# Batch-norm sums in a graph network kernel: the squares and sums of a pair of tiles move one pair later in the order

## The chip, the cores and the metric

The kernel runs on one core of one Trainium2 chip. The metric is device microseconds of one execution. Before the change three runs took 1545.77, 1546.34 and 1549.16 us, so the median is 1546.34 us. The engines are named as in the profile: PE is TensorE (with PEld for its weight loads), DVE is VectorE, ACT is ScalarE, POOL is GpSimd, SP is SyncE, whose queue issues most DMA transfers.

## The reference

The input is a matrix x of 6250 nodes by 256 features and 200,000 edges (src, dst). The part that matters here is the end of it, the batch norm over the nodes and the layer norm of each row:

```python
gc = m @ W_gc + b_gc                       # m: normalised sum over a node's edges
x = gc + (feats @ W_res + b_res)
core = _moe_ff(x, Wg, bg, w1, b1, w2, b2)  # top 2 of 64 experts: g1*y1 + g2*y2 per node
y = x + core
mean = jnp.mean(y, axis=0)
var = jnp.mean((y - mean) ** 2, axis=0)
gnn = (y - mean) * jax.lax.rsqrt(var + BN_EPS) * gamma + beta
out = _layernorm(feats + gnn, axis=-1)
```

The mean and the variance run over all 6250 nodes, so no output row can be finished before the last row of y is known.

## The kernel before, in words

The nodes are cut into NT = 50 tiles of TP = 125 rows. The sums over the edges, the linear layers, the routing and the 64 experts come first and take the span up to about 1418 us. The experts write their results to DRAM (y_dram), two rows of 256 numbers for each node. The pre-expert x of all nodes lies in SBUF in one tile, `x_all`, 125 partitions by 50 by 256, float32.

Then comes the part that the change touches, which I call the batch-norm part. It goes over the 50 tiles in 25 pairs (t0 = 0, 2, 4, ...). For each pair the order in the code is:

- SP issues the load of the pair's expert results from y_dram into a buffer `yr` (512 KB; two loads of half a pair for the first two pairs). There are 8 such buffers, and the loads of later pairs wait until DVE has read the buffer eight pairs before.
- ACT multiplies each tile's second expert row by its gate, in place (L1576, two instructions).
- DVE multiplies each tile's first expert row by its gate and adds it to x (L1578, two instructions), and then adds the gated second rows of both tiles (L1580, one instruction of 512 columns).
- ACT squares the finished pair into a buffer `sq` (L1582, one instruction of 512 columns; 4 such buffers).
- PE adds up x over the 125 rows with a matmul against a matrix of ones, accumulating in PSUM in `pm` (L1584), and likewise `sq` in `pv` (L1586). Each is two matmuls per pair in the code, and each of these stands as two in the trace, so `pm` and `pv` show four matmuls each per pair.

These blocks stand in a `manual_schedule`, which keeps each engine's instructions in the order of the code. An engine works its own list strictly from the front: an instruction that waits holds up everything behind it on that engine. Between engines only the semaphores of the data order the work.

After the last pair the mean is taken from `pm` (L1588), then the variance from `pv` (L1592), and from them `scale` and `less` (L1593 to L1598). The last part (L1622 to L1654) scales every tile, adds the input and the batch norm's shift, does the layer norm and writes the rows out, in groups of up to five tiles. It needs `scale`, so all of it stands behind the sums.

Of the kernel before, what the change touches and what calls it, by code (L numbers as in the profile page):

```python
# [9 lines left out]
F32 = mybir.dt.float32  # L10
# [16 lines left out]
TP = 125  # L27
NT = N // TP
# [3 lines left out]
D = 256  # L32
# [117 lines left out]
def gnn_moe_kernel(ctx, tc, x_in, x_cols, src, dst, bases, nexts, firsts, parts, lasts, W_gc, b_gc, W_res, b_res, Wg, bg, w1, b1, w2, b2,  # L150
# [31 lines left out]
    def node_in(tile_ap, ap, t0, n, end=NT):  # L182

        if t0 + n in (end, NT):
            node_dma(nc.sync, True, tile_ap[:TP, n - 1:n], node_rows(ap, t0 + n - 1, 1))
            n -= 1
        if n:
            loads.append(nc.sync.dma_start(out=tile_ap[:, :n], in_=bass.AP(  # L188
                tensor=ap.tensor, offset=ap.offset + t0 * TP * ap.ap[0][0],
                ap=[[ap.ap[0][0], 128], [TP * ap.ap[0][0], n], [1, ap.shape[1]]])))  # L190
# [1362 lines left out]
    with tc.tile_pool(name="fin", bufs=1) as fp, tc.tile_pool(name="gat", bufs=8) as gp, \  # L1553
# [10 lines left out]
        S.activation(eps[:, 1:2], eps[:, 0:1], AF.Sqrt)  # L1564
        pm = ps_m.tile([TP, D], F32, name="pm")
        pv = ps_m.tile([TP, D], F32, name="pv")
        for t0 in range(0, NT, 2):
            yr = gp.tile([128, 2, 2, D], F32, name="yr")
            for t in range(t0, t0 + 2) if t0 < 4 else (t0,):
                n = 1 if t0 < 4 else 2  # L1570
                loads.clear()
                node_in(yr[:, t - t0:t - t0 + n].rearrange("p t j d -> p t (j d)"), y_rows, t, n)
                for u in written[-AHEAD:-1] if t == 0 else ():
                    tc.add_manual_dep(loads[0].ins, u.name, SYNCED, reason="the last writes")
            for t in range(t0, t0 + 2):
                S.activation(yr[:TP, t - t0, 1, :], yr[:TP, t - t0, 1, :], AF.Copy, scale=gates[:, 1, t:t + 1])  # L1576
            for t in range(t0, t0 + 2):
                V.scalar_tensor_tensor(x[:, t, :], yr[:TP, t - t0, 0, :], gates[:, 0, t:t + 1], x[:, t, :],  # L1578
                                       op0=ALU.mult, op1=ALU.add)
            V.tensor_tensor(x[:, t0:t0 + 2, :], x[:, t0:t0 + 2, :], yr[:TP, :, 1, :], ALU.add)  # L1580
            sq = fl.tile([TP, 2, D], F32, name="sq", bufs=4)
            S.activation(sq, x[:, t0:t0 + 2, :], AF.Square)  # L1582
            for t in range(t0, t0 + 2):
                T.matmul(pm, ones[:TP, :TP], x[:, t, :], start=(t == 0), stop=(t == NT - 1))  # L1584
            for t in range(t0, t0 + 2):
                T.matmul(pv, ones[:TP, :TP], sq[:, t - t0, :], start=(t == 0), stop=(t == NT - 1))  # L1586
        mean = fp.tile([TP, D], F32, name="mean")
        V.tensor_scalar(mean, pm, 1.0 / N, None, op0=ALU.mult)  # L1588
        msq = fp.tile([TP, D], F32, name="msq")
# [12 lines left out]
        groups, t0 = [], 0  # L1602
# [120 lines left out]
```

## Time and profile before

| quantity | value |
|---|---|
| median of three runs | 1546.34 us |
| the profiled execution's own time | 1543.25 us |
| its span, first to last instruction | 1541.5 us |
| mean granted TensorE clock over the span | 0.959 |
| batch-norm part, first gate product to first use of `pv` | 1421.19 to 1479.63 us |
| pairs in it | 25 |
| last part, from the first scaling to the end | 1483.45 to 1541.5 us |

The span is in microseconds from the first instruction. The profiled execution took 3.1 us less than the median of the runs; of its own time 1.75 us lie outside the span. In the batch-norm part the reader should look at four engines at once: ACT and DVE hand each other a pair's data twice, PE only receives, and SP's loads run ahead. POOL does nothing there.

### The profile page before, as it was taken

How to read it: one execution, taken by the hardware profiler on the slowest of the kernel's cores; microseconds unless marked ns; L12 is line 12 of the kernel's file. 1: busy time of each engine (PE TensorE's matmuls, PEld its weight loads, DVE VectorE, ACT ScalarE, POOL GpSimd, SP SyncE). 2: the span in 40 equal slices, each digit the busy share in tenths (PEclk: the TensorE clock that was granted, in tenths of full speed). 3: DMA queues.
4: the chain of work that ended last, by engine and by line, in shares of the span. 5: the costliest groups of instructions: out<-in, count | busy, mean ns of one | idle time of the engine just before them, and what ended most of it. 6: DMA issues, size and time to landing. Idle time of an engine off the chain costs nothing. (4 is left out here: it accounts for less than half of the span.)

```text
span 1541.5 us, 33071 instructions
## 1 busy us (share of the span) xinstructions
PE 1380.2 (90%) x9987; PEld 1147.4 (74%) x9987; DVE 1047.4 (68%) x2943; ACT 745.3 (48%) x1891; POOL 784.1 (51%) x878
## 2 busy tenths in 40 slices
PE   5999478899999999999999967799999999997963
PEld 3555267788888899999999956688888877875642
DVE  9999889989888888888777749333223233222687
ACT  4675544456666566665555524322222222222668
POOL 7000226777776677766666620376566665652000
PEclk9999699999999999999999978899999999998986
DMA  6899665777777787777777737478687887874804
GB/s 192 263 287 327 241 212 162 209 226 224 210 220 221 204 235 214 217 214 219 218 204 216 203 94 245 130 255 268 203 277 253 277 272 219 250 243 152 286 22 147
DMA packets 209177, 336.41 MB, mean 218 GB/s; under 512 B 22283, under 2 KB 140758, under 8 KB 208989
## 3 DMA queue, kind: packets, MB, share of 16 engines
q1 hardware_dynamic: 154201, 180.36, 37.2%
q0 software_dynamic: 47888, 146.77, 32.4%
q10 hardware_dynamic: 6900, 7.07, 1.6%
q8 instruction: 81, 1.33, 0.4%
q14 instruction: 107, 0.88, 0.2%
HBM read 254.55 MB, written 73.10 MB: 213 GB/s over the span
## 5 line engine op out<-in xcount | busy, mean ns | idle before, releaser
L613 POOL DMA_INDIRECT r<-h_dram,srcg x445 | 468.9, 1054 | 244.1 <-PE pc L699 79.4
L745 PE MATMUL sm<-hrow,counts 128*128 128x258 f32 x1470 | 486.9, 346 | 8.4 <-DVE counts L736 8.3
L719 ACT CAST counts<-pc 128x196 f32 (+7 forms) x879 | 356.9, 406 | 209.0 <-PE pc L699 175.0
L746 PE MATMUL sm<-hrow,counts 128*128 128x256 f32 x1470 | 394.6, 282 | 0.0
L699 PE MATMUL pc<-hotk,lo 128*128 128x245 bf16 (+7 forms) x1118 | 305.0, 304 | 41.7 <-DVE counts L736 19.9
L745 PEld LDWEIGHTS sm<-hrow,counts 128*128 128x128 f32 x1470 | 286.6, 195 | 26.4 <-issue 11.9
L686 DVE TENSOR_TENSOR hotk<-key,iota_h 128x784 bf16<-128x784 f16 (+4 forms) x488 | 246.8, 506 | 58.1 <-PE pc L699 56.0
L746 PEld LDWEIGHTS sm<-hrow,counts 128*128 128x128 f32 x1470 | 279.8, 190 | 1.3
L1442 ACT ACTIVATE hT<-ph,b1c 128x112 f32<-128x112 f32 (+16 forms) x256 | 109.9, 430 | 325.4 <-PE ph L1440 309.9
L736 DVE TENSOR_TENSOR counts<-pc,counts 128x49 f32 x908 | 217.6, 240 | 48.8 <-ACT counts L719 12.3
L1452 PE MATMUL py<-w2s,hT 128*128 128x256 f32 (+7 forms) x992 | 238.0, 383 | 0.0
L1440 PE MATMUL ph<-xgT,w1s 128*128 128x112 f32 (+17 forms) x1024 | 203.0, 342 | 0.6 <-DVE xgT L1430 0.6
L1452 PEld LDWEIGHTS py<-w2s,hT 128*128 128x128 f32 (+7 forms) x992 | 161.0, 170 | 42.2 <-DVE ys L1455 2.5
L1440 PEld LDWEIGHTS ph<-xgT,w1s 128*128 128x128 f32 x1024 | 167.7, 192 | 31.1 <-issue 11.2
L1405 POOL DMA_INDIRECT y_dram<-ys,dest x124 | 119.1, 960 | 112.2 <-DVE ys L1455 63.7
L1455 DVE TENSOR_TENSOR ys<-py,b2s 128x256 f32<-128x256 f32 (+7 forms) x124 | 52.3, 422 | 176.9 <-PE py L1452 167.5
L1405 POOL DMA_INDIRECT xg<-x_dram,ids x124 | 120.3, 970 | 91.9 <-DVE ids L1362 52.9
L699 PEld LDWEIGHTS <-lo 128*128 128x128 bf16 x1118 | 99.5, 100 | 74.7 <-issue 17.4
L618 PE MATMUL pg<-r,hot 128*128 128x258 f32 x445 | 144.6, 325 | 3.1 <-DMA r<-h_dram,srcg 2.3
L1430 DVE TENSOR_SCALAR xgT<-pte,bsum 128x112 f32<-128x112 f32 (+14 forms) x128 | 48.8, 423 | 125.9 <-PE pte L1427 125.8
L619 PE MATMUL pg<-r,hot 128*128 128x256 f32 x445 | 125.1, 281 | 0.0
L457 PE MATMUL pr<-wcat,f 128*128 128x512 f32 x196 | 99.6, 632 | 3.2 <-DMA wcat<-in_L_gnn_W_res_dram 3.2
(330 smaller groups left out, 1724.7 us busy)
## 6 DMA issues: line engine op xcount, KB each, us to landing
w1s<-in_L_gnn_w_dram SPq DMA_DIRECT2D x64, 512.0 KB
w2s<-in_L_gnn_w_dram SPq DMA_DIRECT2D x64, 512.0 KB
y_dram<-zeros SPq DMA_DIRECT2D x48, 256.0 KB
yr<-y_dram SPq DMA_DIRECT2D x22, 512.0 KB
b2s<-in_L_gnn_b_dram SPq DMA_DIRECT2D x64, 128.0 KB
h_dram<-hrow SPq DMA_DIRECT2D x5, 1536.0 KB
r<-h_dram,srcg POOLq DMA_INDIRECT x445
f<-in_x_cols_dram SPq DMA_DIRECT2D x25, 256.0 KB
```

The lines of the kernel that those rows point to most:

```text
L613: G.indirect_dma_start(out=f32(r[:, :2 * D]), out_offset=None, in_=h_dram[:, :], in_offset=bass.IndirectOffsetOnAxis(ap=idx, axis=0))
L618: T.matmul(pg, hot, r[:, D:], start=first, stop=False)
L619: T.matmul(pg[:, :D], hot, r[:, :D], start=False, stop=last)
L686: V.tensor_tensor(hot, pairs(key, e, n, m), iota_h[:, None, :m, :].to_broadcast([128, n // 2, m, 2]), ALU.is_equal)
L699: T.matmul(pc, los[g // PAIRS][:, r // 2, :, r % 2], hots.pop(g), start=(i == 0), stop=(i == k - 1))
L719: put = S.copy(counts[c % 2][:, :, 1:][:, :, ds(at, w - 1)], pc[:, :, 1:])
L736: add = V.tensor_tensor(to, more, f32(had), ALU.add).ins
L745: T.matmul(sm, by, hrow[:, t, D:], start=(t == 0), stop=False)
L746: T.matmul(sm[:, :D], by, hrow[:, t, :D], start=False, stop=(t == NS - 1))
L1405: w = G.indirect_dma_start(**kw)
L1440: T.matmul(ph[:, :m], w1s[:, kk, c * 128:(c + 1) * 128], xgT[:, kk, :m], start=(kk == 0), stop=(kk == 1))
L1452: T.matmul(py[:n], hT[:, c, k * 128:k * 128 + n], w2s[:, c, :], start=(c == 0), stop=(c == 3))
```

## The change

The body of the loop is cut in two functions. `joined(t0)` holds the load, the gate products and the sums with x; `summed(t0)` holds the squares and the two sums on PE. The loop now calls `joined` for a pair and then `summed` for the pair before it; the last pair's `summed` comes after the loop. Nothing is computed in another way. The squares have 3 buffers instead of 4.

```diff
-        for t0 in range(0, NT, 2):
+        def joined(t0):
+
             yr = gp.tile([128, 2, 2, D], F32, name="yr")
...
             V.tensor_tensor(x[:, t0:t0 + 2, :], x[:, t0:t0 + 2, :], yr[:TP, :, 1, :], ALU.add)
-            sq = fl.tile([TP, 2, D], F32, name="sq", bufs=4)
+
+        def summed(t0):
+
+            sq = fl.tile([TP, 2, D], F32, name="sq", bufs=3)
             S.activation(sq, x[:, t0:t0 + 2, :], AF.Square)
             for t in range(t0, t0 + 2):
                 T.matmul(pm, ones[:TP, :TP], x[:, t, :], start=(t == 0), stop=(t == NT - 1))
             for t in range(t0, t0 + 2):
                 T.matmul(pv, ones[:TP, :TP], sq[:, t - t0, :], start=(t == 0), stop=(t == NT - 1))
+
+        for t0 in range(0, NT, 2):
+            joined(t0)
+            if t0:
+                summed(t0 - 2)
+        summed(NT - 2)
```

Only ACT's list changes its order. At the start of the batch-norm part, where `yr` is the buffer of a pair's expert results (one number for each pair), `sq` the squares and "x2" two instructions alike, ACT had before:

```order
L1576 ACTIVATE yr_21471<-yr_21471,gates_16387 125x256 x2
L1582 ACTIVATE sq_21479<-x_all_16381 125x512
L1576 ACTIVATE yr_21485<-yr_21485,gates_16387 125x256 x2
L1582 ACTIVATE sq_21493<-x_all_16381 125x512
L1576 ACTIVATE yr_21499<-yr_21499,gates_16387 125x256 x2
L1582 ACTIVATE sq_21506<-x_all_16381 125x512
```

and has now:

```order
L1577 ACTIVATE yr_21471<-yr_21471,gates_16387 125x256 x2
L1577 ACTIVATE yr_21479<-yr_21479,gates_16387 125x256 x2
L1586 ACTIVATE sq_21487<-x_all_16381 125x512
L1577 ACTIVATE yr_21493<-yr_21493,gates_16387 125x256 x2
L1586 ACTIVATE sq_21500<-x_all_16381 125x512
L1577 ACTIVATE yr_21506<-yr_21506,gates_16387 125x256 x2
```

The gate products of the second pair have moved ahead of the first pair's squares, and so on for each later pair: the squares that stand behind a pair's gate products are now those of the pair before. At the end of the part, up to the square root for `scale`, ACT had before:

```order
L1576 ACTIVATE yr_21772<-yr_21772,gates_16387 125x256 x2
L1582 ACTIVATE sq_21779<-x_all_16381 125x512
L1576 ACTIVATE yr_21785<-yr_21785,gates_16387 125x256 x2
L1582 ACTIVATE sq_21794<-x_all_16381 125x512
L1594 ACTIVATE scale_21804<-scale_21804 125x256
```

and has now:

```order
L1577 ACTIVATE yr_21766<-yr_21766,gates_16387 125x256 x2
L1586 ACTIVATE sq_21773<-x_all_16381 125x512
L1577 ACTIVATE yr_21779<-yr_21779,gates_16387 125x256 x2
L1586 ACTIVATE sq_21788<-x_all_16381 125x512
L1586 ACTIVATE sq_21794<-x_all_16381 125x512
L1604 ACTIVATE scale_21804<-scale_21804 125x256
```

Here the squares of the last two pairs stand one behind the other. The lists of PE, DVE and SP hold the same instructions in the same order as before; PE's is two matmuls into `pm` and two into `pv` for each pair, 25 times. The fourth square and those after it now wait for PE to have read the squares three pairs before; it was four.

## The prediction

> **What bounds the kernel now.** I read the chain of waits first, near its end, because the change touches only a stretch close to the end of the program. Columns: start, duration (us), and what stood on the chain.
>
> ```profile
> 1467.73 0.70 DVE x_all L1580
> 1468.48 0.04 issue
> 1468.52 0.63 ACT sq L1582
> 1469.15 0.81 ACT yr L1576 x2
> 1469.96 0.02 issue
> 1469.98 0.70 DVE x_all L1580
> ...
> 1477.47 1.14 PE pm L1584 x4
> 1478.61 0.02 issue
> 1478.63 0.44 DVE mean L1588
> ...
> 1479.63 0.43 DVE scale L1592
> ```
>
> The same three steps come back for every pair: DVE finishes a pair (L1580), ACT squares it (L1582), and only then may ACT make the gate products of the next pair (L1576), which DVE waits for. From 1467.73 to 1469.98 is 2.25 us for one pair. PE is on this chain only behind the last pair, and the mean and `scale` stand directly behind PE. The last part of the kernel needs `scale`, so what the sums gain or lose moves the end of the kernel by as much.
>
> The list of waits between 1434.5 and 1477.47 us says the same in totals (us, times, longest):
>
> ```profile
> ACT sq L1582 <- DVE x_all L1580: 15.8, 19, 1.1
> DVE x_all L1580 <- ACT yr L1576: 14.8, 19, 1.1
> PE pm L1584 <- DVE x_all L1580: 5.2, 20, 0.4
> ```
>
> ACT and DVE wait for each other about 0.8 us in each of 19 pairs, and PE waits for DVE. So no engine is full: the bound is a loop of two engines. The timeline of one pair shows how much work there is apart from the waiting (start, duration, instruction; in brackets the idle time before it and who ended it):
>
> ```profile
> 1433.75 0.69 DVE L1580 TENSOR_TENSOR x_all<-x_all,yr 125x512 f32<-125x512 f32 x1 [0.76 <-ACT yr L1576]
> 1434.36 0.88 DVE L1578 SCALAR_TENSOR_TENSOR x_all<-yr,gates,x_all 125x256 f32<-125x256 f32 x2
> 1434.54 0.63 ACT L1582 ACTIVATE sq<-x_all 125x512 f32<-125x512 f32 x1 [0.82 <-DVE x_all L1580]
> 1435.08 0.89 ACT L1576 ACTIVATE yr<-yr,gates 125x256 f32<-125x256 f32 x2
> 1436.00 0.69 DVE L1580 TENSOR_TENSOR x_all<-x_all,yr 125x512 f32<-125x512 f32 x1 [0.76 <-ACT yr L1576]
> ```
>
> DVE's period is 2.25 us (1433.75 to 1436.00) with 0.76 idle: 1.49 us of work. ACT's is 2.25 with 0.82 idle: 1.43 us of work.
>
> PE's own need is read where PE was behind and worked without a gap, early in the part, from starts and not from ends:
>
> ```profile
> 1428.90 1.03 PE L1584 MATMUL pm<-x_all,ones 125*125 125x256 f32 x4
> 1429.77 1.03 PE L1586 MATMUL pv<-sq,ones 125*125 125x256 f32 x4
> 1430.63 1.03 PE L1584 MATMUL pm<-x_all,ones 125*125 125x256 f32 x4
> ...
> 1434.50 1.13 PE L1584 MATMUL pm<-x_all,ones 125*125 125x256 f32 x4 [0.25 <-DVE x_all L1580]
> ...
> 1477.47 1.13 PE L1584 MATMUL pm<-x_all,ones 125*125 125x256 f32 x4 [0.26 <-DVE x_all L1580]
> ```
>
> Four matmuls take 0.865 us, a pair 1.73 us (1428.90 to 1430.63). So the needs for one pair are PE 1.73, DVE 1.49, ACT 1.43, against 2.25 now.
>
> **The change part by part.** *ACT's order.* Nothing is added or removed; 24 of the 25 squares move behind the gate products of the next pair. The gate products of pair k+1 then no longer stand behind a square that waits for DVE's pair k. What is left of the loop is this: L1580 of pair k, the square of pair k (0.54 us from its start to the next start on ACT, 1434.54 to 1435.08), gate products of pair k+2 (0.89), L1580 of pair k+2 (0.69), with hand-overs of some 0.1: 2.2 us again, but for two pairs, so 1.1 us a pair. That is below the work of each engine alone, so the loop no longer binds. Next in line is the fullest engine, PE with 1.73 us a pair.
>
> *The main term.* The third pair's `pm` starts at 1428.90 and the 25th's at 1477.47: 48.57 us for 22 pairs. At 1.73 us these are 38.06. Gain 10.51 us.
>
> *The start.* The first square now stands behind the gate products of the second pair, and these wait for a load:
>
> ```profile
> 1423.20 0.63 ACT L1582 ACTIVATE sq<-x_all 125x512 f32<-125x512 f32 x1 [0.80 <-DVE x_all L1580]
> 1424.36 0.48 DVE L1578 SCALAR_TENSOR_TENSOR x_all<-yr,gates,x_all 125x256 f32<-125x256 f32 x1 [0.61 <-DMA yr<-y_dram]
> 1423.22 2.07 PE L1584 MATMUL pm<-x_all,ones 125*125 125x256 f32 x4 [9.45 <-DMA yr<-y_dram]
> 1425.09 1.91 PE L1586 MATMUL pv<-sq,ones 125*125 125x256 f32 x4
> 1426.80 1.41 PE L1584 MATMUL pm<-x_all,ones 125*125 125x256 f32 x4
> ```
>
> The second half of pair 2 lands for 1424.36. Its gate product takes 0.4 to 0.5 us (two take 0.89), so the first square starts at about 1424.8 instead of 1423.20 and ends at 1425.4. The first `pv` matmuls, now at 1425.09, start at about 1425.5: PE stands 0.4 us in its list, with everything behind it. PE is slow there anyhow, as its clock shows (columns: window, length, PE busy, granted clock, DMA share, GB/s):
>
> ```profile
> 1426.00:1427.00 1.00, 1.00 (x4) 0.50 0.97 299
> 1427.00:1428.00 1.00, 1.00 (x4) 0.72 1.01 356
> 1428.00:1429.00 1.00, 1.00 (x6) 1.00 1.07 416
> ```
>
> The clock doubles within 1427 to 1428, at about 1427.56 by its mean of 0.72. If it steps at the same time, the 0.4 us of slow work that was put off is done at twice the speed later and costs 0.2. Bounds: 0 (the first pair may be fed in time) and 0.4 (the step moves along). I take 0.2. Between 1428.90 and the end nothing else is late: the later pairs' gate products and squares run at 1.43 to 1.49 us a pair and PE at 1.73, so the lead grows.
>
> *Three buffers of squares in place of four.* ACT's square of pair k waits until PE has read that of pair k-3; behind it on ACT stand the gate products of pair k+2, and DVE's L1580 waits for those. From that release to a finished pair k+2 are 0.54 + 0.89 + 0.69 and about 0.1 for the hand-overs, 2.2 us; PE then still has pairs k-2 to k+1 before it, 4 x 1.73 = 6.9 us. The wait holds ACT and DVE back to PE's pace and PE never sees it. Cost 0. Even a single buffer would leave it two pairs, 3.5 us, as cover; without any the wait would cost up to 2.2 us a pair.
>
> *The loads.* Their number and order on SP's queue stay; the pace at which buffers come free changes.
>
> ```profile
> 1430.00:1440.00 10.00, 9.24 (x41) 7.03 (x40) 6.74 (x15) 6.68 (x15) 0.00 (x0) 1.00 1.05 390
> 1440.00:1450.00 10.00, 8.95 (x37) 6.19 (x35) 6.46 (x13) 6.17 (x14) 0.00 (x0) 1.00 0.77 261
> ...
> SPq L188 <- DVE x_all L1580: 25.7, 15, 1.8
> ```
>
> These rows end in clock, DMA share and GB/s. With buffers free the loads move 390 GB/s. From 1440 on it is 261, and SP's queue waits 25.7 us for DVE to give buffers back, so it is DVE that slows them. A pair of 512 KB (524,288 bytes) takes 1.34 us at 390 and would need 303 GB/s at 1.73 us. Cost 0. If 261 were all that the loads can give, a pair would take 2.0 us from about the 14th pair on; the eight buffers' lead of some 5 pairs over the work covers most of it, and I bound this cost at 11 x (2.0 - 1.73) = 3.0 us.
>
> *The end.* The last pair's L1580 and square are done several us before PE gets to them, so the mean follows PE's last `pm` as it does now. The last part keeps its order. Cost 0.
>
> *Sum.* 10.5 - 0.2 = 10.3 us. The profiled execution, 1543.25 us (span 1541.5), would become 1532.9. It took 3.1 us less than the median of the runs, and no part of that lies in an edit here, so I take the 10.3 off the median: 1546.3 - 10.3 = 1536.0 us, 0.7%.
>
> The row of waits above says that PE idles for only 5.2 us in this stretch, and a reader could take that for all there is to win. The gap of 0.25 us is counted from the modelled end of the matmul before, which shows a latency (four matmuls 1.03 us long start 0.865 apart); the starts tell the pace. The Trainium skill (Perfetto Trace Analysis, section Tensor Engine Instruction (MATMUL, LD_WEIGHTS)) says of these records that the profiler computes the end from the size of the instruction and does not observe it. By starts the sum is 10.5, by the idle rows 5.2; this case's rows agree with the page, since consecutive records overlap.
>
> **The rivals.**
>
> *The clock steps up later.* PE's 0.4 us of idleness falls into the stretch in which the clock is still 0.50. If the wait for full clock began anew at 1425.5, it would last as long as the first time (1423.22 to 1427.56, 4.3 us), until 1429.8: 2.3 us more at half speed, which cost 1.1 us, and with the 0.4 us the gain would be 10.5 - 1.5 = 9.0: 1537.3 us. For it speaks only that PE was busy without a gap before the step in the trace; against it, that 0.4 of 4 us is little. The Trainium skill (TensorE: Matmul & The Clock Gate, section What's actually happening) states that the clock steps up after one busy window of about 3.4 us that runs freely, not counted from the first matmul; by it the step comes at the same time or one window later, for which half of 3.4, an estimate of 1.7 us, would be lost. The 4.3 us from first matmul to step agree with such a window, and no run here shows what a gap in it does.
>
> *The idle rows are right.* If a matmul behind a full queue took the 0.1 us longer that the records after a wait show, PE would need 2.25 - 0.25 = 2.0 us a pair and the gain would be 5.2 less the start: 5.0, so 1541.3 us. Against it: the groups quoted from 1428.90 on start 0.865 us apart, each behind a full queue.
>
> *The loads hold PE up* by the bound above: gain 7.3, so 1539.0 us. Against it: 390 GB/s while buffers were free.
>
> *Slower: the half clock stays.* At clock 0.50 four matmuls take 1.71 us (1425.09 to 1426.80), a pair 3.42. If the broken start left PE at half clock, each us of it would cost half a us, so the gain is gone when the half clock lasts some 20 us longer; if it lasted the whole part, 22 x (3.42 - 2.21) = 26.6 us would be lost: 1573 us. Against it: a PE that is fuller than now, and rows like this one of the middle of the kernel, where PE worked 200 us without a gap at full clock:
>
> ```profile
> 600.00:800.00 200.00, 200.00 (x1544) 188.87 (x1544) 161.85 (x533) 121.78 (x267) 135.67 (x131) 1.00 0.75 214
> ```
>
> *It does not do what it says.* If the squares still stood ahead of the next gate products, nothing would move: 1546. The instruction order excludes that for ACT; what could still do it is a wait that asks for more than its data.
>
> **How the numbers follow.** The forecast, with the start at 0 to 0.4 us, has 0.78. The later clock has 0.07, the loads 0.06, the idle rows 0.04, no effect 0.03, slower 0.02. The predicted time is 1536.0 us. The three runs before lie within 3.4 us, so a median of few runs may be off by 1 to 2 us: the range goes from 1533.5 (gain 10.5 and a low median) to 1539.0 (takes in the later clock and the loads' bound). The chances: a measurement of this kernel tells about 0.2%, 3 us, from no change. All cases but the last two gain more: faster 0.95. No effect stays within it: same 0.03. Slower 0.02.
>
> **What would show it.** Right: the chain no longer has the square between L1580 and the gate products; PE stands on it from the first pairs to the mean; `pm` starts 1.73 us apart from the third pair on; DVE's first use of `pv` comes about 10.3 us earlier after the first gate product than the 58.4 us now (1421.19 to 1479.63); ACT's squares wait for PE in the second half. The start is right if the first `pv` matmul comes 0.3 to 0.5 us later and the clock still steps within the same us. Wrong: `pm` starts 2.0 us apart or more at clock 1.00 (idle rows), gate products that wait for loads after the third pair (loads), a clock of 0.50 beyond 1428.5 (later clock), or a last part that grows.

## The result and the profile after

The changed kernel takes 1535.49 us in the median of six runs (1533.3 to 1537.3), the kernel before 1546.76 us in the median of six (1544.88 to 1549.16). The ratio is 0.9925 with a 95% interval of 0.991 to 0.9939, so the gain is 9 to 14 us. A second comparison on one chip, five runs of the changed kernel against nine of the one before, gave 1537.74 against 1547.12 us, ratio 0.9937 (0.9924 to 0.9951).

The chain of waits in the batch-norm part, in the profiled execution after (start, us, what):

```profile
1422.38 5.26 DMA yr<-y_dram
1427.67 0.51 ACT yr L1577
1428.17 0.53 ACT sq L1586
1428.70 0.04 issue
1428.75 2.07 PE pv L1590 x4
1430.82 0.86 PE pm L1588 x4
1431.68 0.86 PE pv L1590 x4
...
1469.67 0.86 PE pv L1590 x4
1470.53 0.88 PE pm L1588 x4
1471.43 0.44 DVE mean L1598
...
1472.43 0.44 DVE scale L1602
```

The three steps of DVE and ACT that came back in every pair are gone from the chain. From the first `pv` to the mean the chain is PE alone, 0.86 us for each group of four matmuls. The timeline of PE gives the pace by starts:

```profile
1426.26 2.07 PE L1588 MATMUL pm<-x_all,ones 125*125 125x256 f32 x4 [9.91 <-DVE x_all L1581]
1428.75 2.07 PE L1590 MATMUL pv<-sq,ones 125*125 125x256 f32 x4 [0.41 <-ACT sq L1586]
1430.61 1.07 PE L1588 MATMUL pm<-x_all,ones 125*125 125x256 f32 x4
1431.52 1.03 PE L1590 MATMUL pv<-sq,ones 125*125 125x256 f32 x4
1432.38 1.03 PE L1588 MATMUL pm<-x_all,ones 125*125 125x256 f32 x4
...
1470.37 1.03 PE L1588 MATMUL pm<-x_all,ones 125*125 125x256 f32 x4
```

From the third `pm` (1432.38) to the 25th (1470.37) are 37.99 us, 1.727 a pair; before it was 48.57. The windows show PE full, DVE and ACT at most 95% busy, and the loads at 390 GB/s for longer than before (columns: window, length, then busy time and count of PE, PEld, DVE, ACT and POOL, granted clock, DMA share, GB/s):

```profile
1430.00:1440.00 10.00, 10.00 (x46) 8.58 (x46) 9.37 (x19) 9.51 (x21) 0.00 (x0) 0.97 1.05 392
1440.00:1450.00 10.00, 10.00 (x48) 8.68 (x47) 9.37 (x20) 8.84 (x20) 0.00 (x0) 1.00 1.05 387
1450.00:1460.00 10.00, 10.00 (x48) 8.70 (x47) 9.37 (x20) 8.42 (x18) 0.00 (x0) 1.00 0.85 287
```

DVE is closer to its own limit than the 9.37 us suggest. Its last steps of two pairs start 1.59 us apart (L1581, 1434.72 and 1436.31), and it keeps that pace until 1461.73, so it gains only 0.14 us a pair on PE.

The list of waits from 1425 to 1468 us shows what ACT waits for now:

```profile
ACT sq L1586 <- PE pv L1590: 4.0, 11, 1.1
ACT sq L1586 <- DVE x_all L1581: 1.4, 9, 0.2
DVE x_all L1581 <- ACT yr L1577: 0.4, 2, 0.2
```

ACT's and DVE's waits for each other fell from 30.6 us to 1.8 us, over 43 us each, and in 11 pairs, from 1449.85 us on, the square waits for PE to give a buffer back.

I divide the part into the start (first gate product to the third `pm`), the stretch (third to 25th `pm`), and the end (to the first use of `pv`), and put the two profiled executions side by side:

| us | before | after | difference |
|---|---|---|---|
| up to the first gate product | 1421.19 | 1423.08 | +1.89 |
| start | 7.71 | 9.30 | +1.59 |
| stretch, 22 pairs | 48.57 | 37.99 | -10.58 |
| end | 2.16 | 2.06 | -0.10 |
| last part, from the first use of `pv` to the end of the span | 61.87 | 61.87 | 0.00 |
| span | 1541.5 | 1534.3 | -7.2 |

The first row lies ahead of the change. It moves from execution to execution: in the nine profiled executions on chips on which the kernel before takes 1544 to 1547 us it came at 1421.19 to 1425.40 us. Without this row the execution after is 9.1 us shorter (7.2 and 1.9). The two profiled executions took 1543.25 and 1536.07 us, 7.2 us apart, and the medians lie 11.3 us apart; these two profiles do not show where the 2.2 us between 9.1 and 11.3 lie.

### The profile page after: what moved, and what is told of

It is laid out like the page before. It is cut to its first block, busy times and chain, and to the rows that moved or that the text cites. A ratio compares the mean times of both kernels' runs of the same rounds, so it can differ in the third digit from the quotient of the medians.

```text
span 1534.3 us, 33072 instructions
## 1 busy us (share of the span) xinstructions
PE 1376.0 (90%) x9987; PEld 1149.8 (75%) x9987; DVE 1051.2 (69%) x2943; ACT 745.3 (49%) x1891; POOL 780.8 (51%) x878
## 6 DMA issues: line engine op xcount, KB each, us to landing
h_dram<-hrow SPq DMA_DIRECT2D x5, 1536.0 KB
```

## The experiments

Each kernel was profiled once. I compare the three pieces of the part, which do not depend on how late it began. Four of the kernels (half of `pv` in the order before, two pairs behind, the first pair at once, the warm PE) ran on another chip, on which the kernel before took 1613.42 us, so only the pieces of these are used. The two kernels with half of `pv` leave the squares of every second tile out of the variance; they serve to find the bound and nothing else. The last three rows have five runs each, the rows between them and the first two a single one.

| kernel | start | stretch | us a pair | whole part |
|---|---|---|---|---|
| before | 7.71 | 48.57 | 2.21 | 58.44 |
| after | 9.30 | 37.99 | 1.73 | 49.35 |
| after, four buffers | 9.63 | 37.99 | 1.73 | 49.67 |
| before, three buffers | 8.30 | 48.85 | 2.22 | 59.30 |
| after, one buffer | 7.94 | 41.73 | 1.90 | 51.77 |
| after, half of `pv` | 7.81 | 34.64 | 1.57 | 44.61 |
| before, half of `pv` | 7.93 | 49.46 | 2.25 | 59.55 |
| after, two pairs behind | 11.74 | 37.99 | 1.73 | 51.79 |
| after, first pair at once | 8.93 | 37.98 | 1.73 | 48.97 |
| after, warm PE | 8.32 | 37.99 | 1.73 | 48.37 |
| after, once more | 11.22 | 37.99 | 1.73 | 51.27 |
| after, rounded squares | 8.56 | 34.18 | 1.55 | 44.90 |
| after, rounded squares, warm PE | 7.20 | 34.85 | 1.58 | 44.21 |

### The number of buffers, alone

```diff
-            sq = fl.tile([TP, 2, D], F32, name="sq", bufs=3)
+            sq = fl.tile([TP, 2, D], F32, name="sq", bufs=4)
```

> The changed kernel with four buffers of squares again in place of three. Theory (PE sets the pace, the buffers cost nothing): pm starts from the third to the 25th pair 38.0 us, 1.73 us a pair as with three, and ACT's squares wait for PE less often than in 11 pairs; time within 2 us of 1535.5. Rival (three buffers hold the pairs back): a shorter stretch, 36 us or less, and 1533 us or less.

The stretch is 37.99 us to the hundredth, the time 1535.47 us in one run. The square waits for PE in 2 pairs instead of 11, and that changes nothing. The reverse, three buffers in the old order:

```diff
-            sq = fl.tile([TP, 2, D], F32, name="sq", bufs=4)
+            sq = fl.tile([TP, 2, D], F32, name="sq", bufs=3)
```

> The kernel before with three buffers of squares in place of four, order unchanged. Theory (the order of ACT's list sets the pace before, not the buffers): pm starts from the third to the 25th pair 48.6 us as before, time within 2 us of 1546.5. Rival (the number of buffers has a part in the gain): a different stretch by more than 1 us.

The stretch is 48.85 us (48.57 with four), the time 1546.3 in one run. Between three buffers and four, only the order counts.

One buffer tests the reasoning of the prediction on the wait for a buffer, which had found even a single one covered:

```diff
-            sq = fl.tile([TP, 2, D], F32, name="sq", bufs=3)
+            sq = fl.tile([TP, 2, D], F32, name="sq", bufs=1)
```

> The changed kernel with one buffer of squares. The square of a pair then waits until PE has read the pair before. Theory of the prediction: from that release to the next square's end is 0.63 us and some 0.1 of hand-over, while PE has 0.86 us of pm matmuls before it needs it, so PE keeps 1.73 to 1.80 us a pair, a stretch of 38.0 to 39.6 us. Rival (the wait reaches PE): the loop of PE, square, gate products and DVE binds, 2.2 us or more a pair, a stretch of 48 us or more.

Neither: 1.90 us a pair, a stretch of 41.73 us, 1540.79 us in all. The timeline of this kernel shows the loop (DVE's lines and the weight loads left out):

```profile
1449.77 0.81 PE L1590 MATMUL pv<-sq,ones 125*125 125x256 f32 x3
...
1450.41 1.03 PE L1588 MATMUL pm<-x_all,ones 125*125 125x256 f32 x4
1450.66 0.63 ACT L1586 ACTIVATE sq<-x_all 125x512 f32<-125x512 f32 x1 [0.47 <-ACT yr L1577]
...
1451.34 1.13 PE L1590 MATMUL pv<-sq,ones 125*125 125x256 f32 x4
...
1452.56 0.63 ACT L1586 ACTIVATE sq<-x_all 125x512 f32<-125x512 f32 x1 [0.47 <-ACT yr L1577]
...
1453.24 1.13 PE L1590 MATMUL pv<-sq,ones 125*125 125x256 f32 x4
```

The brackets name ACT's own instruction before the square, but that had ended at 1450.19, 0.47 us earlier: what the square waits for is PE. The square starts 1.22 us after the start of `pv` (1451.34 to 1452.56): four matmuls that follow a wait stand at 1.13 us to their modelled end, and 0.09 us more pass until ACT starts. With 0.63 us for the square and 0.05 us to the next `pv` that is 1.90 us. The expectation had counted the matmuls at their pace of 0.86 us; who waits for them to finish has to count their length. The prediction's "two pairs, 3.5 us, as cover" for a single buffer is wrong for another reason: it followed the wait only through the gate products to the `pm` two pairs later. But the square itself is what the very next `pv` needs, and only that pair's `pm`, 0.86 us, lies between. With three buffers PE has two pairs more to do in between, and nothing of the wait shows.

### Less work on PE, in the new order and in the old

```diff
-            for t in range(t0, t0 + 2):
-                T.matmul(pv, ones[:TP, :TP], sq[:, t - t0, :], start=(t == 0), stop=(t == NT - 1))
+            T.matmul(pv, ones[:TP, :TP], sq[:, 0, :], start=(t0 == 0), stop=(t0 == NT - 2))
```

> The changed kernel without the pv matmuls of the second tile of each pair: the squares of half of the tiles are left out of the variance. PE then needs 1.30 us a pair. Theory (PE sets the pace, DVE is next): pm starts fall to DVE's pace, 1.5 to 1.6 us a pair, a stretch of 33 to 35.2 us, and DVE shows hardly any idle time. Rival (loads are next): the stretch falls less or not at all, and gate products wait for loads after the third pair. Rival (the loop of ACT and DVE still sets the pace): 38 us.

With a quarter of PE's work gone the pairs come 1.57 us apart, the stretch is 3.4 us and the part 4.7 us shorter. The timeline shows that DVE is the next bound: its instructions stand without a wait in the list, and it is PE's weight loads that wait for DVE.

```profile
1446.54 0.69 DVE L1581 TENSOR_TENSOR x_all<-x_all,yr 125x512 f32<-125x512 f32 x1
...
1447.15 0.87 DVE L1579 SCALAR_TENSOR_TENSOR x_all<-yr,gates,x_all 125x256 f32<-125x256 f32 x2
1447.28 0.72 PEld L1588 LDWEIGHTS pm<-x_all,ones 125*125 125x125 f32 x4 [0.43 <-DVE x_all L1581]
...
1448.12 0.69 DVE L1581 TENSOR_TENSOR x_all<-x_all,yr 125x512 f32<-125x512 f32 x1
```

DVE's own need is 1.58 us a pair (1446.54 to 1448.12), not the 1.49 that I had read as period less idle time. DVE's last step starts 0.97 us after the start of the two before it when it follows them directly (1447.15 to 1448.12), although these take 0.87.

The same cut in the old order, with the same edit:

> The kernel before without the pv matmuls of the second tile of each pair: the squares of half of the tiles are left out of the variance. PE's need falls from 1.73 to 1.30 us a pair. Theory (before, the loop of ACT and DVE sets the pace, PE none): 2.21 to 2.25 us a pair from the third pair to the 25th, 48.6 us or up to 1 us more since PE has no backlog to work off at the start; end of the part 0.4 us earlier at most. Rival (PE's matmuls behind a wait have a share in it): 2.0 us a pair or less.

The pace is 2.25 us, no better than the 2.21 over the same pairs before, where the first of them ran at PE's pace from a backlog. The list of waits between 1501.7 and 1551 us of this kernel, 49 us where the prediction's list spans 43:

```profile
ACT sq L1582 <- DVE x_all L1580: 18.2, 22, 1.1
DVE x_all L1580 <- ACT yr L1576: 17.0, 22, 1.1
PE pm L1584 <- DVE x_all L1580: 14.4, 21, 0.8
```

PE's idle time grew from 5.2 us in 43 to 14.4 us in 49, and nobody gained by it. A quarter of PE's work is worth 3.4 us of the stretch in the new order and nothing in the old: the bound did move from the loop of DVE and ACT to PE.

### How far behind

```diff
         for t0 in range(0, NT, 2):
             joined(t0)
-            if t0:
-                summed(t0 - 2)
+            if t0 > 2:
+                summed(t0 - 4)
+        summed(NT - 4)
         summed(NT - 2)
```

> The changed kernel with the squares and sums two pairs behind the gate products instead of one. Theory (PE sets the pace): the same 1.73 us a pair; the first pv matmul comes later by the gate products and the load of one more pair, 0.5 to 1.5 us, so the part is as long as with one or up to 1 us longer. Rival (what is left of the loop still holds the pairs back): a stretch shorter than 37.5 us.

The stretch is again 37.99 us. The first `pv` comes 2.38 us after PE was free for it, and the start is 11.74 us. The part is 2.4 us longer than with one pair, where at most 1 was expected: besides the wait, PE's clock was still at half until about 1500.98, 8.8 us after the first matmul. Nothing is left to win by distance in the stretch. That the start pays for it fits the 2.38 us of waiting, but one execution does not show how much: the starts of the unaltered changed kernel alone differ by 1.9 us (9.30 and 11.22).

```diff
             joined(t0)
-            if t0:
+            if t0 == 0:
+                summed(0)
+            elif t0 > 2:
                 summed(t0 - 2)
```

> The changed kernel with the first pair's squares and sums at once, and from the second pair on one pair behind. Theory (the wait for the second pair's load costs 0.4 us of PE at half clock, worth 0.2): PE has no gap between the first pm and the first pv matmul; 1.73 us a pair; the part 0.1 to 0.5 us shorter for the same landing of the loads. Rival (the gap puts the clock's step off): the clock steps up earlier after the first matmul than the 4.4 us with the gap, by 2 us or more.

The gap ahead of the first `pv` is gone, the start is 8.93 us against 9.30, the part 0.38 us shorter. That is of the size expected, but the loads' landing moves by as much between executions, so it is not shown. The clock stepped up 4.9 us after the first matmul, not earlier than the 4.4 us with the gap of 0.41.

```diff
+        warm = ps_f.tile([TP, 5, D], F32, name="pf", padded_shape=[TP, 6, D])
+        for _ in range(11):
+            T.matmul(warm[:, 0, :], ones[:TP, :TP], gam, start=True, stop=True)
+
         def joined(t0):
```

> The changed kernel with eleven more matmuls of 256 columns on PE, into a PSUM buffer that nobody reads, ahead of the first pm, where PE has no work for some 6 us. Theory: PE is at full clock when the first pair comes, each group of four takes 0.86 us from the start, and PE is fed at DVE's pace until the backlog is there: third pm 1 to 2 us earlier after the first gate product, then 1.73 us a pair; the part 1 to 2 us shorter. Rival (loads, not the clock, set the start): the part as long as before this edit, within 0.3 us.

The start is 8.32 us, the part 48.37, about 1 us shorter than after; 1 to 2 were expected. With starts of 9.30 and 11.22 us in two executions of the unaltered changed kernel, 1 us in one execution is not shown either. The eleven matmuls took 6.71 us and ran until the first `pm`, which came 4.5 us after the first gate product (3.2 after). So PE was at full clock but began later, and I read this as a share of the saving lost.

### The same kernel timed again, and two with less work for PE

> The changed kernel unaltered, timed beside the two below on one chip: 0.991 to 0.994 of the kernel before; 1.73 us a pair from the third pair to the 25th, a stretch of 38.0 us; first gate product to first use of pv 48.5 to 50 us.

The stretch repeats to the hundredth, and the ratio of 0.9937 lies in the range expected. But the profiled execution had a start of 11.22 us, so its part of 51.27 us missed the 48.5 to 50 expected. PE's timeline shows why, and below it the windows from 7 us after the first matmul on (columns: window, length, PE busy, granted clock, DMA share, GB/s):

```profile
1430.87 2.07 PE L1590 MATMUL pv<-sq,ones 125*125 125x256 f32 x4 [1.04 <-ACT sq L1586]
1432.73 1.91 PE L1588 MATMUL pm<-x_all,ones 125*125 125x256 f32 x4
1434.44 1.80 PE L1590 MATMUL pv<-sq,ones 125*125 125x256 f32 x4
```

```profile
1434.75:1435.75 1.00, 1.00 (x4) 0.50 1.05 385
1435.75:1436.75 1.00, 1.00 (x6) 0.88 1.06 391
```

The second pair's load landed late, PE stood for 1.04 us in its list, and the clock stepped up only at about 1435.99: 8.2 us after the first matmul, 5.1 after the restart. This is what the rival "the clock steps up later" warned of, in an execution of the unaltered changed kernel.

The next kernel gives PE less work without leaving out a tile, by a type for the squares whose matmuls stand in the trace once instead of twice:

```diff
+        ones_r = fp.tile([TP, TP], F32R, name="ones_r")
+        V.tensor_copy(ones_r, ones[:TP, :TP])
...
-            sq = fl.tile([TP, 2, D], F32, name="sq", bufs=3)
+            sq = fl.tile([TP, 2, D], F32R, name="sq", bufs=3)
...
-                T.matmul(pv, ones[:TP, :TP], sq[:, t - t0, :], start=(t == 0), stop=(t == NT - 1))
+                T.matmul(pv, ones_r, sq[:, t - t0, :], start=(t == 0), stop=(t == NT - 1))
```

> The changed kernel with the squares and a copy of the matrix of ones in the rounded 32-bit type in which the edge sums before already work (one matmul on PE instead of two); the squares lose some of their last bits, the sums of x do not. PE's need falls to some 1.3 us a pair. Theory (PE sets the pace, DVE is next at 1.59 us): a stretch of 34.6 to 35.0 us and 3.0 to 3.4 us less than the changed kernel, 0.989 to 0.991 of the kernel before. Rival (the loads or ACT are next): a stretch above 36 us, 1.5 us less or none.

It takes 1530.13 us in the median of five runs, ratio to the kernel before 0.9898 (0.9883 to 0.9913), and beats both kernels: the interval lies below that of the changed kernel on the same chip. DVE sets its pace, 1.58 us a pair once a backlog of the first pairs is worked off (1.55 over the whole stretch), and PE waits for DVE in each of the later pairs:

```profile
1441.35 0.69 DVE L1583 TENSOR_TENSOR x_all<-x_all,yr 125x512 f32<-125x512 f32 x1
1441.96 0.88 DVE L1581 SCALAR_TENSOR_TENSOR x_all<-yr,gates,x_all 125x256 f32<-125x256 f32 x2
...
1442.10 1.13 PE L1590 MATMUL pm<-x_all,ones 125*125 125x256 f32 x4 [0.22 <-DVE x_all L1583]
```

The stretch is 34.18 us, 3.8 less than after, a little more than the 3.0 to 3.4 expected. The medians lie 7.6 us apart, more than twice what was expected. In the profiled executions 2.7 us lie in the start (8.56 us against 11.22). That a PE with spare time works off a late clock step would fit, since the clock stepped late here too, 6.5 us after the first matmul; it is not shown apart from where the loads landed. How much of the remaining us is scatter is open.

The last kernel adds a warm PE to it, with fewer matmuls:

```diff
+        warm = ps_f.tile([TP, 5, D], F32, name="pf", padded_shape=[TP, 6, D])
+        for _ in range(6):
+            T.matmul(warm[:, 0, :], ones[:TP, :TP], gam, start=True, stop=True)
```

> The kernel above with six more matmuls of 256 columns on PE ahead of the first pm, whose result nobody reads, so that PE's clock is up when the first pair comes. Theory: with PE below DVE's need the start is set by loads and DVE, so a warm PE saves 0.3 to 1 us more at most: third pm up to 1 us earlier after the first gate product, a stretch of 34.6 to 35.0 us, 0.988 to 0.991 of the kernel before. Rival (the half clock sets the start): 1.5 us or more.

The start is 7.20 us, 1.4 shorter than without the six matmuls, where at most 1 was expected; the stretch is 0.7 us longer and the part 44.21, 0.7 us shorter. The time does not show it: 1531.91 us, ratio 0.9904 (0.9891 to 0.9918), an interval that overlaps the one without.

## Why the prediction was right

**The bound and its shift: right.** The loop of L1580, squares and gate products was the bound. The two kernels with half of `pv` show it from both sides, and the chain after is PE from the first `pv` to the mean.

**The main term: right.** 10.51 us predicted, 10.58 measured, and 37.98 or 37.99 us for the stretch in all six runs that keep PE's work, one pair behind or two, with three buffers or four.

**The idle rows: refuted as a price.** Two us a pair were the other reading of "PE idle 5.2 us". The pace is 1.727, 0.52 less than the 2.25 before, so the 0.25 us of idleness per pair showed only half of what PE had to spare. The page of the Trainium skill that the prediction names (Perfetto Trace Analysis, section Tensor Engine Instruction (MATMUL, LD_WEIGHTS)) agrees: ends of matmuls are modelled. For a reader that waits for the result the length does count, as the one buffer shows.

**The start: the term was too small.** The term was 0.2 us, with 0.4 as its bound. In the profiled execution the start was 1.59 us longer than before, and it splits at the first `pm`. Up to there ACT, DVE and PE have the same work in both kernels, yet it took 3.18 us from the first gate product, against 2.03 before. The second half of the first pair landed later, as the gate product that waited for it shows (the kernel before, then the one after; their first gate products start at 1421.19 and 1423.08):

```profile
1421.89 0.51 ACT L1576 ACTIVATE yr<-yr,gates 125x256 f32<-125x256 f32 x1 [0.20 <-DMA yr<-y_dram]
1424.92 0.51 ACT L1577 ACTIVATE yr<-yr,gates 125x256 f32<-125x256 f32 x1 [1.33 <-DMA yr<-y_dram]
```

So 1.15 us of the 1.59 are where loads landed and not the new order. The other 0.44 us lie between the first `pm` and the third, 6.12 us against 5.68. Here the prediction's steps came true: PE stood 0.41 us ahead of the first `pv`, and the clock stepped 4.42 us after the first matmul, against 4.34 before. The price was the bound of 0.4 and not the 0.2; that half of the gap would be won back at the doubled clock did not show. Other executions paid more. From the first `pm` to the third took 7.11 us with four buffers, where the gap was 0.72 us, and 8.32 us in the repeated run, with a gap of 1.04; the old order with three buffers took 5.83. What was mis-sized is the landing of the second pair's load, which had been taken from one execution: there it came 3.17 us after the first gate product, after the change 4.59 (1423.08 to 1427.67) and, in the repeated run, 4.94 (1424.85 to 1429.79). The old order was less exposed, because its first square did not wait for this load.

**The later clock: a rival with 0.07 that takes place in some executions.** In the repeated run the way from the first `pm` to the third was 2.6 us longer than before; the rival had priced 1.5. It does not replace the forecast, it takes a share of the gain from it. Its mechanism, a wait that begins anew behind the gap, is not what the traces show; the last section has what they do.

**Buffers and loads: right at their cost of 0.** The loads gave 392 and 387 GB/s where 303 were needed, and three buffers had the stretch of four. DVE's need was 0.1 us a pair larger than read, with no effect while PE is the bound.

**The sum: right, its closeness in part by luck.** 10.3 us predicted; the medians moved by 11.3 and 9.4 us, and both intervals hold 10.3. The part itself was 9.1 us shorter in the profiled execution, where the prediction's sign asked for about 10.3; with the 1.15 us of the loads set aside it is 10.2. The last part is unchanged at 61.87 us, so the gain reached the end undiminished. That 1536.0 and 1535.49 us lie so close is partly luck, since two comparisons of the same kernels differ by 1.9 us.

## What to carry to other kernels

When two engines hand the same data to and fro and a third only receives it, try moving the receiver's feed one step behind in the list of the engine that waits. Here the pace then fell to the work of the fullest engine, read from starts where that engine had a backlog. One step of distance was enough; with two the stretch was the same, and the start was longer in the one execution. After such a change look at the new bound at once: taking a quarter of PE's work away was worth nothing before the change and 3.4 us of the stretch after it.

## What the runs showed of the hardware

The clock's step to full speed came at very different times after PE's first matmul of the part, though PE had been idle for 9 to 10 us before it. It took 3.4, 3.5, 4.3, 4.65, 4.9 and 5.4 us in runs in which PE then worked without a gap, and 3.5 and 5.8 us in the two with extra matmuls, idle for some 5 us before. With a gap of 0.41 us it took 4.4 us. With gaps of 0.72, 1.04, 1.19 and 2.38 us it took 6.1, 8.2, 6.5 and 8.8 us.

The length of the gap is not what orders these times; the granted clock shows a grid. In all 13 profiles the spell at half clock around the start lasted 6.83, 10.24 or 13.65 us, which is two, three or four times 3.41 us. In the repeated run, for one, the mean clock of 0.67 from 1422 to 1423 us puts its beginning at 1422.34, and its end is the 1435.99 found above. Counted back from the step in pieces of 3.41 us, PE was busy for 0.88 or more of the last piece in every profile, and for 0.70 or less of every earlier piece of the spell. The pieces with the gap, in the changed kernel and then in its repetition (columns: window, length, PE busy, granted clock, DMA share, GB/s):

```profile
1427.27:1430.68 3.41, 3.00 (x8) 0.50 1.02 351
1429.16:1432.58 3.42, 2.38 (x6) 0.50 1.02 362
```

The first, 0.88 busy, ended with the step. The second, 0.70 busy, did not, and the step came one piece later. On these figures a gap counts by what it leaves of such a piece, and where the piece begins is not set by the first matmul. Where between 0.70 and 0.88 the limit lies these runs do not tell. The Trainium skill (TensorE: Matmul & The Clock Gate, section What's actually happening) speaks of a window of about 3.4 us that runs freely and has to be a busy one. The traces agree, with pieces of 3.41 us. The times without a gap, 3.4 to 5.8 us, agree too: one whole window after the wait for its beginning gives, as an estimate by that page, 3.4 to 6.8 us.
